# A transformer layer on one core: first row's transposes and weight pieces, last group's softmax and residual loads moved

## The chip, the core and the metric

The kernel runs on one core of a Trainium2 chip. The core has a matrix engine (TensorE, PE in the profile; its weight loads are PEld), a vector engine (VectorE, DVE), an activation engine (ScalarE, ACT), a general engine (GpSimd, POOL) and a queue engine (SyncE, SP) that issues most of the transfers. The engines run side by side and wait for each other by semaphores; each works through its own list of instructions in order. [...]

The metric is the device time of one execution in microseconds (us), as the median of three runs. Besides, one execution was taken with the hardware profiler; it has a time of its own.

## The reference

The input `x` is 16 rows of 512 tokens with 512 features. Attention and a gated feed-forward part both read the same normalised input, and both are added to `x`:

```python
xn = layernorm(x)
q, k, v = split(xn @ w_qkv.T + b_qkv)              # 16 heads of 32
p = softmax(q @ k.T / sqrt(32) + causal)
attn = (p @ v) @ w_out.T + b_out
g = (xn @ gate_w.T) * gate_s                       # 1408 wide, weights -1, 0, 1
u = (xn @ up_w.T) * up_s
ffn = ((silu(g) * u) @ down_w.T) * down_s
out = x + attn + ffn
```

## The kernel before

Precision is kept by splitting float32 values into two float16 halves, a high one and the rest (`xh`, `xl`, `wq_h`, `wq_l`, `qkh`, `qkl`, `hh`, `hl`, `oh`, `ol`), so that each product is two or three matmuls of 128 x 512. ACT usually writes the high half, DVE or POOL the rest.

The 16 batch rows are handled one after the other, and in each the 16 heads in four groups of four. One group of one row is a slot: 64 slots, numbered 0 to 63. In a slot the softmax of the group runs (`soft_run`): PE computes scores in three blocks, for query tile 3, for tile 2, and for tiles 1 and 0 together, in four score banks (tag `s1`); DVE masks them and takes the maximum (L556), ACT the exponential (L561), ACT and DVE split the result (L581, L586), and SP issues DMA transposes of it (L595). In the next slot `av_step` multiplies with the values: PE spreads the reciprocal sums into a tile `R` (L628), ACT copies it to `Rs` (L631), PE does the product `av` (L641), DVE scales it (L654), ACT and POOL split it into `oh` and `ol` (L655, L656; five buffers each).

Between these, PE is filled with other work (`fillers`): the query and key projections of the next group (`qk_proj`, two tiles, out through ACT at L464), the value projections of a row, the chunks of the feed-forward part (`ffn_chunk`, a `g` and a `u` tile of eight matmuls each; chunks 0 to 2 in the first slot of a row, 3 and 4 in the second, 5 to 10 in the third), the four down tiles (`down_tile`, 22 matmuls each, fourth slot), and the four output tiles of the row before (`out_tile`, 12 matmuls each, second slot). These tiles share three PSUM banks (tag `mm`): a new tile can start when the third tile before it has been read. The output tiles of the last row (`ends`) start with three head groups and are finished with the fourth at the very end.

Who comes when is decided by a planner (`Plan.order`). Each step has an engine, a planned duration and the things that it reads and writes. PE takes, of the steps that can start, the one with the lowest key; keys are spread over the slot by `place`. The other engines take the one that has been ready longest, moved by its `slack` (a negative one makes it earlier). The outcome is one fixed list per engine. The table of planned times is used for nothing else.

At the start, SP loads the first row (four tiles of 256 KB) and the projection weights (twelve pieces of 256 KB: query, key and value part, four pieces of the contraction each, L263). DVE computes the statistics and normalises (L375 to L393), PE transposes the normalised row in four groups of four (`ln_tr`, L423) into `mm` banks, ACT and DVE split each group into `xh` and `xl` (L428, L431), and ACT and DVE split each weight piece (L270, L273). Then the projections of group 0 begin. For the later rows the transposes are done by DMA.

At the end of each row, `down_tile` brings a tile out of PSUM (L713), loads the residual again into a single buffer (`xr`, L716), and POOL adds the output bias to it and it to the tile (L717, L718). The output tile is then added on DVE (L739) and stored (L742).

## Time and profile before

| what | value |
|---|---|
| median of three runs | 1915.01 us (1914.96 to 1915.26) |
| the profiled execution's own time | 1915.52 us |
| its span, first to last instruction | 1913.7 us |
| PE, DVE, ACT, POOL busy | 98%, 77%, 70%, 51% of the span |
| first matmul (a transpose) of PE | 11.29 us |
| last matmul of PE | starts 1904.69 us |
| last instruction of DVE | starts 1905.18 us |

Times in the profile count from the start of the span. A row of the timeline has the start, the duration, the engine, the line and operation, what it writes and reads, how often, and in brackets how long the engine had idled and what ended it. Buffer numbers are left out, so `qk` stands for any projection tile. Matmuls overlap: the distance from start to start (about 0.22 us for 128 x 512 at full clock) tells the pace, not the duration. The granted clock is the clock that PE was allowed, 1.00 being full. POOL's spans are rough.

### The profile page before, as it was taken

What the parts mean: (1) busy time and instruction counts of PE and PEld (TensorE: products, weight loads), DVE (VectorE), ACT (ScalarE), POOL (GpSimd) and SP (SyncE); (2) the same over time, 40 slices, a digit from 0 to 9 for tenths busy, and PEclk for the clock granted to TensorE, in tenths of its full rate; (3) what the DMA queues carried; (4) which work ended last, traced back from release to release, by engine and by line L of the source; (5) the groups of instructions that cost most, each with busy time, mean ns of one, the idle gap of its engine ahead of it and who ended that gap; (6) DMA issues with size and microseconds to landing.
All of it is one profiled execution on the core that took longest, in us unless ns stands there. A gap on an engine that the chain in (4) does not pass through costs nothing. (4 is left out here: it accounts for less than half of the span.)

```text
span 1913.7 us, 40913 instructions
## 1 busy us (share of the span) xinstructions
PE 1877.3 (98%) x15250; PEld 892.2 (47%) x15250; DVE 1482.0 (77%) x3541; ACT 1335.2 (70%) x3185; POOL 983.5 (51%) x713
## 2 busy tenths in 40 slices
PE   7899999999999999999999999999999999999997
PEld 3344444444444444444444444444444444444443
DVE  7778778797887978878788787877869787686674
ACT  5766757677676776767767676776767767677673
POOL 4446455464554646456464554645546454564533
PEclk9999999999999999999999999999999999999999
DMA  9875757666676656767567586667766667666465
GB/s 169 144 127 120 133 128 154 129 130 121 132 153 128 145 109 138 143 135 144 110 133 144 122 148 123 139 121 140 153 127 135 119 136 148 127 130 106 97 118 115
DMA packets 769519, 252.39 MB, mean 132 GB/s; under 512 B 734368, under 2 KB 738848, under 8 KB 769312
## 3 DMA queue, kind: packets, MB, share of 16 engines
q1 hardware_dynamic: 764688, 247.54, 65.7%
q0 software_dynamic: 4624, 2.16, 1.4%
q8 instruction: 121, 1.98, 0.4%
q14 instruction: 86, 0.70, 0.1%
HBM read 55.85 MB, written 16.78 MB: 38 GB/s over the span
## 5 line engine op out<-in xcount | busy, mean ns | idle before, releaser
L561 ACT ACTIVATE p<-s,negm 128x512 f32<-128x512 f32 (+3 forms) x1024 | 529.0, 531 | 231.3 <-DVE negm L556 229.1
L586 DVE SCALAR_TENSOR_TENSOR pq<-p,pq 128x2048 f16<-128x2048 f32 (+3 forms) x256 | 425.7, 1676 | 238.5 <-ACT pq L581 229.2
L556 DVE CUSTOM_DVE_ANT_0 s<-s,mask 128x512 f32<-128x512 f32 (+3 forms) x1024 | 473.1, 517 | 53.0 <-PE s L527 45.2
L581 ACT ACTIVATE pq<-p 128x2048 f16<-128x2048 f32 (+3 forms) x256 | 324.0, 1291 | 10.3 <-DMA pT<-pq 8.4
L691 POOL TENSOR_TENSOR hl<-ft,hh 128x512 f16<-128x512 f32 x176 | 226.9, 1295 | 190.1 <-ACT hh L690 189.3
L469 POOL TENSOR_TENSOR qkl<-qkt,qkh 128x512 f16<-128x512 f32 x128 | 165.1, 1290 | 244.7 <-ACT qkh L467 233.9
L251 PE MATMUL g<-xh,wg 128*128 128x512 f16 x704 | 267.6, 380 | 4.3 <-ACT qkt L464 2.4
L251 PE MATMUL u<-xh,wu 128*128 128x512 f16 x704 | 266.9, 379 | 2.8 <-DVE ft L681 1.5
L251 PE MATMUL dn<-wd,hh 128*128 128x512 fp8e4 x704 | 268.2, 381 | 0.0
L251 PE MATMUL dn<-wd,hl 128*128 128x512 fp8e4 x704 | 267.4, 380 | 0.0
L251 PE MATMUL g<-xl,wg 128*128 128x512 f16 x704 | 266.9, 379 | 0.0
L251 PE MATMUL u<-xl,wu 128*128 128x512 f16 x704 | 266.8, 379 | 0.0
L690 ACT CAST hh<-ft 128x512 f16<-128x512 f32 x176 | 109.3, 622 | 170.5 <-DVE ft L687 170.3
L618 POOL TENSOR_SCALAR rb<-rden 128x512 f32<-128x512 f32 x64 | 137.7, 2151 | 175.9 <-DVE rden L615 175.9
L251 PEld LDWEIGHTS <-wu 128*128 128x128 fp8e4 x1408 | 137.1, 98 | 169.7 <-issue 5.6
L561 ACT ACTIVATION_READ_ACCUMULATOR p<-s,negm 128x1 f32 x1024 | 214.5, 209 | 0.0
L251 PEld LDWEIGHTS <-wg 128*128 128x128 fp8e4 x1408 | 132.6, 98 | 159.6 <-issue 10.3
L251 PEld LDWEIGHTS <-wq_h 128*128 128x128 f16 x1024 | 95.4, 98 | 133.8 <-issue 28.5
L677 ACT ACTIVATE ft<-g,gt_c 128x512 f32<-128x512 f32 x176 | 121.1, 688 | 43.7 <-PE g L251 43.1
L407 POOL TENSOR_TENSOR xnl<-xc,xnh 128x512 f16<-128x512 f32 x60 | 96.7, 1612 | 104.5 <-DMA xl<-xnl 58.4
L687 DVE SCALAR_TENSOR_TENSOR ft<-u,gu_c,ft 128x512 f32<-128x512 f32 x176 | 132.0, 750 | 21.4 <-PE u L251 5.5
L717 POOL TENSOR_TENSOR xr<-xr,bo_b 128x512 f32<-128x512 f32 x64 | 94.4, 1475 | 103.9 <-DMA xr<-in_x 103.9
(114 smaller groups left out, 3205.3 us busy)
## 6 DMA issues: line engine op xcount, KB each, us to landing
xc<-in_x SPq DMA_DIRECT2D x64, 256.0 KB, 4.0
xr<-in_x SPq DMA_DIRECT2D x64, 256.0 KB, 2.9
out<-y SPq DMA_DIRECT2D x64, 256.0 KB, 2.5
pT<-pq SPq DMA_TRANSPOSE x256, 5.5
wq<-in_wqkvT SPq DMA_DIRECT2D x12, 256.0 KB, 5.4
exact<-in_wdT SPq DMA_DIRECT2D x11, 256.0 KB, 2.9
exact<-in_wgT SPq DMA_DIRECT2D x8, 256.0 KB, 3.0
exact<-in_wuT SPq DMA_DIRECT2D x8, 256.0 KB, 2.9
```

The costliest lines, as they stand in the source:

```text
L251: nc.tensor.matmul(ps(), l, r, start=(first + k == 0), stop=(first + k == n - 1))
L407: add("POOL", gps(512), lambda: nc.gpsimd.tensor_tensor(l(), xc(), h(), ALU.subtract), r=[xc, h], w=[l], slack=2)
L469: "POOL", gps(512), lambda: nc.gpsimd.tensor_tensor(l(), t(), h(), ALU.subtract),
L556: nc.vector.tensor_tensor_reduce(sc, sc, mask[:, 512 - n :], -(2.0 ** -7), 3e38, ALU.add, ALU.min, negm()[:, m : m + 1])
L561: nc.scalar.activation(exps(i).rearrange("p (k j) q -> p k j q", j=4)[:, :, j, :], part().rearrange("p (k q) -> p k q", q=P), AF.Exp, bias ...
L581: "ACT", act(4 * n), lambda src=src, half=half: nc.scalar.mul(half(0), src(), 2.0 ** 15),
L586: lambda src=src, half=half: nc.vector.scalar_tensor_tensor(half(1), src(), 2.0 ** 15, half(0), ALU.mult, ALU.subtract),
L618: lambda: nc.gpsimd.tensor_scalar(rb().rearrange("p (c d) -> p c d", d=32), rden().unsqueeze(2).to_broadcast([P, 16, 32]), 2.0 ** -15, Non ...
L677: "ACT", act(512) + 0.1, lambda: nc.scalar.activation(t(), pg(), AF.Tanh, scale=gt_c[:, ic : ic + 1]),
L687: lambda: nc.vector.scalar_tensor_tensor(t(), pu(), gu_c[:, ic : ic + 1], t(), ALU.mult, ALU.mult),
L690: add("ACT", act(512), lambda: nc.scalar.copy(hh(), t()), r=[t], w=[hh], slack=3)
L691: add("POOL", gps(512), lambda: nc.gpsimd.tensor_tensor(hl(), t(), hh(), ALU.subtract), r=[t, hh], w=[hl])
```

## The change

1. `ln_tr` puts its four tiles into the score banks (tag `s1`, four of them) instead of the three `mm` banks, and its ACT and DVE steps get a slack of -8.
2. The query and key weights are loaded and split in two pieces each: first the 128 columns of group 0 for the whole contraction, then the other 384 columns. The value weights come in two pieces of two contraction tiles. There are six loads and six splits instead of twelve; the bias load comes after the first two. The projections wait for the pieces accordingly.
3. For the last row, only two output tiles of the row before are computed in its second slot, the other two in its fourth.
4. In the last slot the keys of the softmax steps are spread over 0.4 of the slot; the last `av` gets a key at 0.6 of it, ahead of the last parts of the output tiles, which begin at the end of the slot.
5. For the last row, the residual tiles lie in the row buffers (tag `xc`, four) instead of one buffer, and are loaded once slot 61 has begun instead of after the down tile.

In the lists that the planner makes, everything between the first projections and slot 61 is the same on every engine. PE's list from slot 61 on, with the number of matmuls (`s1_3`, `s1_2`, `s1_1` are score blocks; slot numbers where it matters):

```
before: av(60) op 8 s1_2 op 28 s1_1 op 8, g u 3 and 4 (32), s1_3(62) qk 24 flagT R av(61) flagR g u 5 ..
        .. g u 10, s1_3(63) R dn 30 av(62) dn 12 s1_2 dn 36 s1_1 dn 10 op 35 R av(63) op 12
after:  av(60) s1_2 op 20 g 4 s1_1 g 4 u 8 g u 4 (16) qk 12 s1_3(62) qk 12 R g 5 s1_2 flagT u 5 av(61) flagR ..
        .. g u 10, s1_3(63) op 24 s1_2 R dn 8 av(62) dn 8 s1_1 dn 50 R dn 22 op 9 av(63) op 27 op 12
```

```diff
-    def load_wqkv(part, kc, t):
+    def load_wqkv(part, k, t, cols, kcs=slice(0, KC)):
+
+        src = wqkvT[kcs.start * P : kcs.stop * P, part * 512 + cols.start : part * 512 + cols.stop]
         add(
             "SP", 0.5,
-            lambda: nc.sync.dma_start(t()[:, kc, :], wqkvT[kc * P : (kc + 1) * P, part * 512 : part * 512 + 512]),
-            w=[(t, kc)], lat=1.3,
-        )
...
+            lambda: nc.sync.dma_start(t()[:, kcs, cols], src.rearrange("(k p) f -> p k f", p=P)),
+            w=[(t, k)], lat=5.2 * (cols.stop - cols.start) * (kcs.stop - kcs.start) / 2048,
+        )
...
+        h, l = wq_h[:, kcs, dst], wq_l[:, kcs, dst]
+        add("ACT", act(n), lambda: nc.scalar.mul(h, t()[:, kcs, cols], 256.0), r=[(t, k)], w=[("wqh", part, k)])
...
+            lambda: nc.vector.scalar_tensor_tensor(l, t()[:, kcs, cols], 256.0, h, ALU.mult, ALU.subtract),
+            r=[(t, k), ("wqh", part, k)], w=[("wql", part, k)], slack=4,
...
-        ps = mm(f"lnT_{b}_{kc}")
+        ps = Tile(pp, [P, 512], F32, "s1", 4, f"lnT_{b}_{kc}")
...
-        add("ACT", act(512), lambda: nc.scalar.copy(xh()[:, kc, :], ps()), r=[ps], w=[(xh, kc)])
+        add("ACT", act(512), lambda: nc.scalar.copy(xh()[:, kc, :], ps()), r=[ps], w=[(xh, kc)], slack=-8)
...
-            r=[ps, (xh, kc)], w=[(xl, kc)],
+            r=[ps, (xh, kc)], w=[(xl, kc)], slack=-8,
...
-                    [(wt, which, kc)] + xtok(b, xx, kc),
+                    [(wt, which, min(g, 1))] + xtok(b, xx, kc),
...
-                    [(wt, 2, kc)] + xtok(b, xx, kc, tb),
+                    [(wt, 2, kc // 2)] + xtok(b, xx, kc, tb),
...
-        xr = work(f"xr_{b}_{tb}", "xr", 1)
+
+        xr = work(f"xr_{b}_{tb}", "xr", 1) if b + 1 < NB else work(f"xr_{b}_{tb}", "xc", 4)
...
-        add("SP", 0.5, lambda: nc.sync.dma_start(xr(), x[b, tb * P : (tb + 1) * P, :]), r=[y], w=[xr], lat=1.3)
+        add(
+            "SP", 0.5, lambda: nc.sync.dma_start(xr(), x[b, tb * P : (tb + 1) * P, :]),
+            r=[y] if b + 1 < NB else [f"slot{NSLOT - 3}"], w=[xr], lat=1.3,
+        )
...
-                step.key = t0 + AV_LAG + (k - 1) * 1.5
+                step.key = t0 + AV_LAG + (k - 1) * 1.5 if s < NSLOT else t0
...
-        if g == 1 and b > 0:
-            for tb in range(NT):
+
+        late = 2 if b == NB - 1 else NT
+        if b > 0 and g in (1, 3):
+            for tb in range(late) if g == 1 else range(late, NT):
                 out_tile(f, b - 1, tb)
...
-    for part in range(3):
-        for kc in range(KC):
-            load_wqkv(part, kc, wst[part])
-        if part == 1:
+    first, others, both = slice(0, P), slice(P, 512), slice(0, 512)
+    pieces = [(0, 0, wst[0], first), (1, 0, wst[1], first), (0, 1, wst[0], others), (1, 1, wst[1], others)]
+    pieces += [(2, k, wst[2], both, slice(2 * k, 2 * k + 2)) for k in range(2)]
+    for n, piece in enumerate(pieces):
+        load_wqkv(*piece)
+        if n == 1:
             add("SP", 0.5, lambda: nc.sync.dma_start(bqk_c, bqk), w=["bqk"], lat=0.3)
...
-    for part in range(3):
-        for kc in range(KC):
-            split_wqkv(part, kc, wst[part])
+    for piece in pieces:
+        split_wqkv(*piece)
...
-        place(start, T)
+
+        place(start, T if s + 1 < NSLOT else 0.4 * T)
         f.place(start, T)
+        early = start + 0.6 * T
...
-    attention_slot(NSLOT)(start, 0.0)
+    attention_slot(NSLOT)(early, 0.0)
...
-    f.place(start + AV_LAG + 4.0, f.total)
+    f.place(start, f.total)
```

More of the change, by code (lines that the diff above doesn't have):

```diff
@@ L257, in mm_group, with split_wqkv @@
             prev = [f.pe(MM4 / 4 * (k1 - k0), lambda k0=k0, k1=k1: run(k0, k1), reads, [ps], prev)]
-    def load_wqkv(part, kc, t):
+    def load_wqkv(part, k, t, cols, kcs=slice(0, KC)):
+        src = wqkvT[kcs.start * P : kcs.stop * P, part * 512 + cols.start : part * 512 + cols.stop]
         add(
             "SP", 0.5,
-            lambda: nc.sync.dma_start(t()[:, kc, :], wqkvT[kc * P : (kc + 1) * P, part * 512 : part * 512 + 512]),
-            w=[(t, kc)], lat=1.3,
-        )
-    def split_wqkv(part, kc, t):
-        cols = slice(part * 512, part * 512 + 512)
-        h, l = wq_h[:, kc, cols], wq_l[:, kc, cols]
-        add("ACT", act(512), lambda: nc.scalar.mul(h, t()[:, kc, :], 256.0), r=[(t, kc)], w=[("wqh", part, kc)])
-        add(
-            "DVE", dve(512),
-            lambda: nc.vector.scalar_tensor_tensor(l, t()[:, kc, :], 256.0, h, ALU.mult, ALU.subtract),
-            r=[(t, kc), ("wqh", part, kc)], w=[("wql", part, kc)],
+            lambda: nc.sync.dma_start(t()[:, kcs, cols], src.rearrange("(k p) f -> p k f", p=P)),
+            w=[(t, k)], lat=5.2 * (cols.stop - cols.start) * (kcs.stop - kcs.start) / 2048,
+        )
+    def split_wqkv(part, k, t, cols, kcs=slice(0, KC)):
+        n = (cols.stop - cols.start) * (kcs.stop - kcs.start)
+        dst = slice(part * 512 + cols.start, part * 512 + cols.stop)
+        h, l = wq_h[:, kcs, dst], wq_l[:, kcs, dst]
+        add("ACT", act(n), lambda: nc.scalar.mul(h, t()[:, kcs, cols], 256.0), r=[(t, k)], w=[("wqh", part, k)])
+        add(
+            "DVE", dve(n),
+            lambda: nc.vector.scalar_tensor_tensor(l, t()[:, kcs, cols], 256.0, h, ALU.mult, ALU.subtract),
+            r=[(t, k), ("wqh", part, k)], w=[("wql", part, k)], slack=4,
         )
@@ L776, in weight_exact @@
         )
-    rng_src = [(wq_h, kc, 512 * k, ("wqh", k, kc)) for k in range(3) for kc in range(KC)]
-    rng_src += [(wo_h, kc, 0, ("woh", kc)) for kc in range(KC)]
+    rng_src = [(wq_h, kc, 512 * k, [("wqh", k, 0), ("wqh", k, 1)]) for k in range(3) for kc in range(KC)]
+    rng_src += [(wo_h, kc, 0, [("woh", kc)]) for kc in range(KC)]
     rng_cols = {38: (0, 4), 39: (4, 8), 40: (8, 12), 41: (12, 16), 35: (16, 28), 36: (28, 40), 37: (40, 51)}
@@ L788, in weight_range @@
             ),
-            r=[tok] + when, w=["ranges"], slack=8,
+            r=tok + when, w=["ranges"], slack=8,
         )
```

## The prediction

> **What bounds the kernel now.** I read the page's busy rows first, then who TensorE waited for, then the order of time at both ends, then the granted clock by stretches.

> ```profile
> PE 1877.3 (98%) x15250; PEld 892.2 (47%) x15250; DVE 1482.0 (77%) x3541; ACT 1335.2 (70%) x3185; POOL 983.5 (51%) x713
> ```

> TensorE (PE) is the bound: it works in all but 36 us of 1913.7. So the change is worth what it takes from PE's idle or slow time.

> ```profile
> PE lnT L423 <- DVE xc L393: 11.3, 1, 11.3
> PE R L628 <- POOL rb L618: 2.9, 1, 2.9
> PE g L251 <- ACT qkt L464: 2.4, 1, 2.4
> PE op L251 <- ACT oh L655: 1.5, 1, 1.5
> PE op L251 <- POOLq L1113: 1.3, 1, 1.3
> PE lnT L423 <- DVE xl L431: 0.8, 1, 0.8
> ```

> These are PE's waits over the span (total, times, longest). The 0.8 is at the head, 1.5 and 1.3 are at the tail; 2.9 and 2.4 lie between, where the order is untouched.

> ```profile
> 14.84 1.28 DVE L431 TENSOR_TENSOR xl<-lnT,xh 128x512 f16<-128x512 f32 x2
> 15.57 1.12 PE L423 MATMUL lnT<-ident,xc 128*128 128x128 f32 x4 [0.82 <-DVE xl L431]
> 16.48 1.91 PE L251 MATMUL qk<-xh,wq_h 128*128 128x512 f16 x4
> 18.19 1.80 PE L251 MATMUL qk<-xl,wq_h 128*128 128x512 f16 x4
> 19.83 1.03 PE L251 MATMUL qk<-xh,wq_l 128*128 128x512 f16 x4
> ```

> The head. The fourth transpose group waits 0.82 us for VectorE (DVE) to free the first of three banks. The next eight matmuls start 0.43 us apart, and from 19.83 on 0.22 apart: PE runs at half speed until about 19.7.

> ```profile
> 1897.82 0.29 PE L641 MATMUL av<-pT,vh 128*32 128x256 f16 x4 [0.85 <-DMA pT<-pq]
> 1900.85 0.39 PE L251 MATMUL op<-wo_h,oh 128*128 128x512 f16 x1 [1.52 <-ACT oh L655]
> 1902.74 0.39 PE L251 MATMUL op<-wo_h,ol 128*128 128x512 f16 x1 [1.29 <-POOLq L1113]
> 1903.24 2.63 DVE L739 SCALAR_TENSOR_TENSOR y<-op,y 128x512 f32<-128x512 f32 x4 [3.10 <-PE op L251]
> ```

> The tail: three waits on the last group's softmax, transposes and split, 0.85 + 1.52 + 1.29 = 3.66 us. After them come twelve matmuls, four additions and the stores.

> ```profile
> 57.24:60.65 3.41, 1.75 (x11) 0.96 (x9) 2.58 (x6) 3.00 (x6) 1.51 (x2) 1.00 0.65 146
> 111.85:115.26 3.41, 0.85 (x4) 0.20 (x2) 3.41 (x8) 1.07 (x4) 1.59 (x2) 1.00 0.27 52
> 115.26:118.67 3.41, 3.05 (x10) 1.59 (x11) 2.73 (x6) 3.41 (x8) 1.43 (x2) 0.51 0.00 0
> ```

> Stretches (PE's busy us first, granted clock third from the end). After a stretch in which PE worked 25%, the clock is 0.51 for 3.4 us; after one of 51% it stays 1.00.

> **The change, part by part: the head.** The four transpose groups get the four score banks, so the wait goes. The third group ends near 14.75; the fourth starts there instead of at 15.57, and the first projection matmul at 15.69 instead of 16.48. Gain 0.8, if its data keep up: group four ends 15.87, ScalarE's (ACT) copy (0.58) 16.5, DVE's difference (0.68) 17.2; matmuls four and eight need them at 17.0 and 18.7 at half speed. DVE is ready, because seven weight splits ahead of and between the four differences became two.

> The loads: 4 MB of input and weights still pass, cut otherwise. The two first pieces have runs of 512 B. Here 256 KB with 2 KB runs took about 0.65 us once flowing (390 GB/s at 9 to 12 us). [...] the pieces, issued from 2.62 on and landing 4.8 to 6.2 after issue, are there at 8 to 10 us. No row here shows a plain 512 B load; if a run cost as much as one of 2 KB, each piece took 2.6 and the second landed at 11.7. ACT needs both split (0.63 each) before its copy at 13.08. So both ends cost nothing and I take nothing. The slack that covers this is under 1 us at the late end; past it, each us is a us on PE. The other pieces are needed from 16.5 on (a 128x1536 ACT split 1.48, DVE 1.76 each), and PE asks for them after 21: hidden. A bias load moves up one place; it is needed at 12.5.

> The half-speed stretch is the open term. [...] 115.26 lies 28.0 windows after 19.69, and the clock's fall at 1907.26 lies 553.0 after it. So the window that opened it was 16.28 to 19.69; the one before (12.87 to 16.28) had the 0.82 hole in it and was 76% busy. With the hole closed it is full, mostly of transposes, and neither page nor trace says what a transpose counts. If it opens at 16.28, eight matmuls take 8 x 0.2155 + 0.3 = 2.0 instead of 3.35: head gain 0.8 + 1.3 = 2.1. If not, the opening stays at 19.69 and the earlier start only adds slow time: gain 0.4. By the row alone (0.43 for the first eight matmuls, wherever they start) it would be 0.8. I take 2.1.

> Two later stretches hang on the same windows, since everything behind the head shifts by its gain. Shifted by 2.1, PE's 2.9 us hole at 112.7 to 115.6 spreads over two windows (about 60% and 54% busy): the slow stretch would go, worth half of its 3.05 busy us, 1.5. But the 2.4 hole at 59.0 to 61.4 then leaves 43% in its window, between the 51% that stayed open and the 36% (1903.85 to 1907.26) after which it closed: up to 1.7 lost. I count the two as zero and keep -1.5 and +1.7.

> **The tail.** Half of the previous row's output tiles (24 matmuls, 24 x 0.2155 = 5.2 us) move from slot 61 into slot 63, between the last group's first and second score blocks; slot 63's blocks come in 0.4 of its length; the last av goes behind the last down tile and nine output matmuls, ahead of 27 others. Counting from the last group's first scores: second block at 6.0, third at 12.6, its exponentials (ACT 3.2 in all) done by about 19, both DVE splits (1.25 + 0.68) by 22.2, transposes landed 5.0 later as at the end of this trace (1892.7 to 1897.7), at 27. PE reaches av at 31.5: no wait (0.85 gone, 4 us to spare). Then 0.68 + 0.62 + 1.15, with hand-overs 2.9 us, lie beside 27 x 0.2155 = 5.8 of PE: 1.52 and 1.29 gone. Gain 3.66.

> What comes late instead is slot 62. With 5.2 us less PE work in slot 61, ACT falls behind. In the order that the planner writes out for the changed kernel, PE has there, from the end of slot 61's av (1815.98) to u of chunk 5, 84 matmuls (18.1), four score blocks (0.69 + 0.70 + 0.85 + 0.69) and two transposes (0.7): it arrives at 1837.7. That tile's bank is held by the second projection of the last group, freed by ACT (L464). ACT is fed last by PE's u of chunk 3 (DVE done 1826.1), then has a projection to wait for (1831.4), 0.72 + 0.51 + 0.52 + three exponentials 0.67, Rs 0.5, one more 0.8, the 128x2048 scaling 1.81 and the projection's own 0.70:

> ```profile
> 1839.30 1.94 ACT L581 ACTIVATE pq<-p 128x2048 f16<-128x2048 f32 x1
> 1841.11 0.70 ACT L464 ACTIVATE qkt<-qk,bqk_c 128x512 f32<-128x512 f32 x1
> ```

> (There 1.81 from start to start.) It ends at about 1839.1, so PE waits about 1.4 (0.5 to 2.9). Queued behind it: u, av, chunk 6. From there on ACT and DVE are ahead again. One or two more switches between kinds of matmul, 0.1 at each side: 0.2.

> Residuals: four loads move from the last group's transfers to slot 61 and into row buffers that are free since slot 56. On SP's queue they stand ahead of slot 61's transposes, whose data come 8 us later; on POOL four additions (1.3 to 1.5) stand ahead of a projection split that PE needs 14 us later (done 1817.7, needed 1831). Two stores stand ahead of the last group's transposes and are due 4 us before them. ACT's `oh` of group 1 now waits for the moved tiles' reads (five buffers), about 4.2 us into slot 63, where ACT is at 4.4. Each costs nothing; POOL's cover is 13 us.

> Sum: head -2.1, windows 0, tail -3.66 + 1.4 + 0.2 = -2.0: -4.1. From the profiled execution's 1915.52 (its span 1913.7) that is 1911.4; the median of the runs lies 0.5 below it: **1910.9**.

> **Rivals.** (1) The clock opens at 19.69 as before: head -0.4, total -2.4, 1912.6. For it: transposes start 0.28 apart[...]. Against: the stretch from 115.26 reopened the clock with R's transposes in it. (2) The wait in slot 62 takes the place of those at the end: if ACT is 3.5 late rather than 1.4, the tail gives nothing, and with the head's 2.1 it is 1912.9. For it: ACT has no idle time there; against: every term is a measured row. (3) Slower: the first pieces land late. ACT is in order, its copy of the first transpose stands behind the second split, and PE behind the copy. Each us after 12.4 costs one; from 16.5 it eats the gain, from 20.3 the kernel is over 0.2% slower (1919). Against: that is eight times what the row gives for the bytes.

> **Chances.** Main case 0.52, (1) 0.33, (2) 0.10, (3) 0.05. Tell-apart bound 0.2% = 3.8 us. The main case passes it in about seven of ten (its own range 1909.0 to 1912.6), (1) in one of seven, (2) in one of ten: faster 0.44, slower 0.06 with (3), within it 0.50. Range: down to 1908.3 (both windows' gain, no wait in slot 62), up to 1914.6 ((1) or (2) with the long wait).

> **What would show it.** No wait of the transposes on `xl`, first projection matmul near 15.7; starts 0.22 apart from 16.3, or from 19.7; the granted clock near 57 and 115. In slot 62 a wait of u on `qkt` of 1 to 2 us; no waits of av or op at the end, and the last matmul 4 us earlier. Wrong if the first pieces land after 12.4, or if slot 61 to 63 holds other waits of over 1 us.

## The result and the profile after

The changed kernel takes 1909.15 us (median of ten executions, 1906.54 to 1911.35), the kernel before, on the same chip, 1914.95 us (1912.92 to 1915.53). The ratio of the two is 0.9972 (95% interval 0.9962 to 0.9982), so the gain is 5.4 us, 3.4 to 7.3. The profiled execution's own time is 1909.74 us and its span 1908.0 us. A second series with the same kernel gave 0.9970 (0.9958 to 0.9982).

The busy row of the page and the waits of TensorE over the span (total, times, longest):

```profile
PE 1877.7 (98%) x15250; PEld 893.3 (47%) x15250; DVE 1485.7 (78%) x3535; ACT 1334.9 (70%) x3179; POOL 986.7 (52%) x713
```

```profile
PE lnT L426 <- DVE xc L396: 10.1, 1, 10.1
PE g L251 <- ACT qkt L467: 3.3, 1, 3.3
PE R L631 <- POOL rb L621: 2.9, 1, 2.9
PE u L251 <- ACT qkt L467: 2.7, 2, 1.7
```

PE's busy time has not moved (1877.3 before): the gain is idle time. The waits on `xl`, on `oh`, on `ol` and on the last `pT` are gone from the list. The wait of `g` has grown from 2.4 to 3.3, and `u` waits 2.7 in two places, 1.7 of it in slot 62. The first matmul starts at 10.1 instead of 11.3; how much of that is chance is said below.

The head in order of time:

```profile
10.09 4.22 PE L426 MATMUL lnT<-ident,xc 128*128 128x128 f32 x16 [10.09 <-DVE xc L396]
14.15 1.21 PE L251 MATMUL qk<-xh,wq_h 128*128 128x512 f16 x4
15.20 1.02 PE L251 MATMUL qk<-xl,wq_h 128*128 128x512 f16 x4
16.06 1.03 PE L251 MATMUL qk<-xh,wq_l 128*128 128x512 f16 x4
```

Sixteen transposes run without a gap, and the projections are at full clock (four in 0.86) from 15.2 on; before, this began at 19.83.

Slot 62 and the end, from the same view:

```profile
1833.66 1.91 ACT L584 ACTIVATE pq<-p 128x2048 f16<-128x2048 f32 x1
1835.47 0.67 ACT L467 ACTIVATE qkt<-qk,bqk_c 128x512 f32<-128x512 f32 x1
1836.19 0.38 PE L251 MATMUL u<-xh,wu 128*128 128x512 f16 x1 [1.65 <-ACT qkt L467]
...
1890.80 0.29 PE L644 MATMUL av<-pT,vh 128*32 128x256 f16 x4
...
1893.47 0.62 ACT L658 CAST oh<-Rs 128x512 f16<-128x512 f32 x1 [8.62 <-DVE Rs L657]
...
1894.16 1.16 POOL L659 TENSOR_TENSOR ol<-Rs,oh 128x512 f16<-128x512 f32 x1 [3.17 <-ACT oh L658]
...
1899.31 2.63 DVE L746 SCALAR_TENSOR_TENSOR y<-op,y 128x512 f32<-128x512 f32 x4 [5.88 <-PE op L251]
1900.03 2.27 SPq L749 DMA_DIRECT2D out<-y  x4
```

The new wait of `u` is 1.65 us, behind the 128x2048 scaling and the projection's exit. At the end `av` has no bracket, so no wait of it shows. `oh` and `ol` are done at 1895.3; of PE's 39 output matmuls after `av` only the last twelve need them, and these start near 1898.4. The table of stretches (PE's busy us first, granted clock third from the end):

```profile
55.06:58.47 3.41, 0.19 (x1) 0.00 (x0) 3.26 (x8) 3.00 (x8) 2.18 (x2) 1.00 0.62 130
58.47:61.88 3.41, 3.33 (x8) 1.16 (x8) 3.20 (x12) 3.41 (x10) 1.25 (x2) 0.50 0.91 169
109.67:113.08 3.41, 0.49 (x4) 0.28 (x4) 3.41 (x10) 1.65 (x5) 1.82 (x2) 1.00 0.03 6
113.08:116.49 3.41, 3.41 (x12) 1.42 (x11) 2.08 (x4) 3.41 (x7) 0.79 (x1) 0.50 0.05 10
1833.40:1836.81 3.41, 1.76 (x17) 0.71 (x17) 2.22 (x9) 3.38 (x6) 0.00 (x0) 1.00 0.41 77
1836.81:1840.22 3.41, 3.41 (x30) 1.43 (x32) 3.41 (x4) 3.38 (x10) 2.35 (x1) 0.50 0.00 0
```

Three stretches of 3.41 us run at half clock, each after one with a wait in it. The kernel before had one, at 115. The third comes behind the new wait in slot 62.

### The profile page after: what moved, and what is told of

It reads as the page before. It is cut to its first block, busy times and chain, and to the rows that moved or that the text cites. A ratio compares the mean times of both kernels' runs of the same rounds, so it can differ in the third digit from the quotient of the medians.

```text
span 1908.0 us, 40895 instructions
## 1 busy us (share of the span) xinstructions
PE 1877.7 (98%) x15250; PEld 893.3 (47%) x15250; DVE 1485.7 (78%) x3535; ACT 1334.9 (70%) x3179; POOL 986.7 (52%) x713
## 5 line engine op out<-in xcount | busy, mean ns | idle before, releaser
L251 PE MATMUL g<-xh,wg 128*128 128x512 f16 x704 | 268.4, 381 | 5.0 <-ACT qkt L467 3.3
L251 PE MATMUL u<-xh,wu 128*128 128x512 f16 x704 | 267.4, 380 | 4.5 <-ACT qkt L467 2.7
L251 PE MATMUL dn<-wd,hh 128*128 128x512 fp8e4 x704 | 268.3, 381 | 0.0
L251 PE MATMUL g<-xl,wg 128*128 128x512 f16 x704 | 267.8, 380 | 0.0
L251 PE MATMUL dn<-wd,hl 128*128 128x512 fp8e4 x704 | 267.6, 380 | 0.0
L251 PE MATMUL u<-xl,wu 128*128 128x512 f16 x704 | 267.6, 380 | 0.0
L251 PEld LDWEIGHTS <-wu 128*128 128x128 fp8e4 x1408 | 137.5, 98 | 171.6 <-issue 8.1
L251 PEld LDWEIGHTS <-wg 128*128 128x128 fp8e4 x1408 | 132.9, 98 | 160.9 <-issue 12.3
L251 PEld LDWEIGHTS <-wq_h 128*128 128x128 f16 x1024 | 95.1, 98 | 132.9 <-issue 26.7
L659 POOL TENSOR_TENSOR ol<-Rs,oh 128x512 f16<-128x512 f32 x64 | 98.8, 1544 | 96.7 <-ACT oh L658 96.6
```

The costliest lines, as they stand in the source:

```text
L251: nc.tensor.matmul(ps(), l, r, start=(first + k == 0), stop=(first + k == n - 1))
L659: add("POOL", gps(512), lambda: nc.gpsimd.tensor_tensor(ol(), r(), oh(), ALU.subtract), r=[r, oh], w=[ol])
```

## The experiments

Each kernel was timed beside the kernel before. The ratio is its time to that kernel's time. Line numbers in the profile of an experiment are those of its own text and differ from the changed kernel's by a few.

| kernel | median us | before us | ratio (95%) |
|---|---|---|---|
| e1_head | 1911.07 | 1913.89 | 0.9985 (0.9979 to 0.9992) |
| e2_tail | 1911.32 | 1913.89 | 0.9985 (0.9978 to 0.9991) |
| e3_banks | 1911.17 | 1913.89 | 0.9986 (0.9979 to 0.9993) |
| e4_pieces | 1913.35 | 1913.89 | 0.9996 (0.9988 to 1.0004) |
| e5_residual | 1913.88 | 1913.54 | 1.0004 (0.9995 to 1.0012) |
| e6_no_late | 1909.85 | 1913.54 | 0.9981 (0.9974 to 0.9988) |
| e7_no_keys | 1912.83 | 1913.54 | 0.9999 (0.9991 to 1.0007) |
| e8_chunk | 1907.21 | 1913.54 | 0.9971 (0.9959 to 0.9982) |
| f_after | 1909.47 | 1913.91 | 0.9970 (0.9958 to 0.9982) |
| e9_warm | 1907.19 | 1913.91 | 0.9962 (0.9949 to 0.9976) |
| e10_both | 1904.89 | 1913.91 | 0.9946 (0.9933 to 0.9960) |
| e11_all | 1902.06 | 1913.91 | 0.9936 (0.9922 to 0.9949) |

The profiles let two lengths be read apart from the rest: from the first transpose to the first scores (the head), and from a projection matmul of slot 61 (at 1811.1 in the kernel before) to the last matmul (the tail).

| kernel | first transpose | clock opens behind it | head | half-clock stretches | tail | last matmul to end of span |
|---|---|---|---|---|---|---|
| before | 11.29 | 8.45 | 15.54 | 115 | 93.59 | 9.0 |
| after | 10.09 | 4.00 | 12.98 | 58, 113, 1837 | 93.04 | 7.2 |
| f_after | 10.81 | 3.39 | 12.70 | 59, 113, 1837 | 93.03 | 7.4 |
| e1_head | 10.80 | 5.05 | 13.31 | 60 | 93.53 | 7.0 |
| e2_tail | 10.99 | 8.28 | 15.45 | 115, 1839 | 93.09 | 7.9 |
| e3_banks | 10.30 | 4.83 | 14.06 | 60 (two), 1899 | 95.17 | 7.0 |
| e4_pieces | 11.06 | 4.04 | 15.12 | none | 93.67 | 8.9 |
| e5_residual | 10.31 | 4.93 | 13.25 | 60, 114 | 90.94 | 12.6 |
| e6_no_late | 10.39 | 6.51 | 14.03 | 112 (two) | 92.53 | 7.9 |
| e7_no_keys | 10.96 | 6.45 | 13.99 | 113 (two) | 94.02 | 6.8 |
| e8_chunk | 9.99 | 4.74 | 13.15 | 59, 114 | 89.58 | 6.7 |
| e9_warm | 10.25 | 5.70 | 13.25 | 13, 112 | 91.40 | 7.3 |
| e10_both | 10.37 | 5.17 | 13.25 | 12, 111 (two) | 89.58 | 8.9 |
| e11_all | 10.50 | 5.56 | 13.25 | 13 | 89.58 | 8.7 |

Half-clock stretches are given by the time at which they begin, "(two)" where it lasts 6.83 us and not 3.41. In the last three kernels the clock had opened before the first real transpose and closed again (below); the table has its second opening. Up to slot 61 PE's order is the same in all kernels but e3_banks, the added transposes aside.

**Head and tail, each alone**

```diff
 e1_head: changes 1 and 2 (banks with their slack, pieces); the rest as before
 e2_tail: changes 3, 4 and 5 (moved output tiles, keys, residuals); the rest as before
```

> The head alone (score banks, pieces, slack); the tail as before. Theory: the head gives 1.2 us (the row's third tile lands earlier), 0.8 (the wait on xl) and about 1.5 (TensorE's full clock one window of 3.41 us earlier), less what later slow windows take: 1911.5 us (1910.5 to 1912.7), first transpose near 10.1, no slow wait in slot 62. Rival, only the wait counts: -0.8, 1914.1. Rival, the gain is the tail's: 1914.9.

> The tail alone (late output tiles, early keys and av, residuals in the row buffers); the head as before. Theory: 3.66 us of waits at the end go, a wait of u on qkt of 1.4 to 1.7 in slot 62 comes, sometimes with a slow clock window after it (up to 1.7): -1 to -2.3, 1912.6 to 1913.9. Rival, the head gives only its 0.8 and the tail the rest: -5, 1910. Rival, the new wait and window eat the tail's gain: 1914.9.

Head alone gives 2.9 us (1.5 to 4.0), tail alone 2.9 (1.7 to 4.2), together 5.8 against 5.4 for the whole. The two halves add, and neither carries the gain by itself. The rivals by which one half gives nothing fall.

**The head taken apart**

```diff
 e3_banks: twelve loads and splits as before, and
-        ps = mm(f"lnT_{b}_{kc}")
+        ps = Tile(pp, [P, 512], F32, "s1", 4, f"lnT_{b}_{kc}")
 with slack=-8 on the ACT and DVE steps behind
 e4_pieces: the six loads and splits, the transposes in the mm banks and without the slack
```

> The score banks and the slack for the first row's transposes alone, with the twelve weight loads as before. Theory: the wait on xl goes (0.8), first transpose still near 11.3, the window without the hole opens the clock earlier in part of the executions: -0.8 to -2.1, 1912.9 to 1914.1. Rival, the twelve weight splits in ACT's and DVE's lists make the projections wait in place of the transposes: 1914.9.

> The weight pieces alone, the transposes in the three banks as before. Theory: the pieces with runs of 512 B leave the row's third and fourth tile more of the transfer rate, so that the third statistic starts near 5.2 instead of 6.5 and the first transpose near 10.1; the wait on xl stays or shrinks: -1.2, 1913.7 (1912.7 to 1914.2). Rival, the earlier landing was chance: first transpose near 11.3, 1914.9.

By the timing the banks with their slack give as much as the whole head (0.9986 against 0.9985), and the pieces alone nothing that can be measured. But e3_banks is not the banks alone: with the twelve loads the planner orders PE's work otherwise from 22 to 118 us, and there the waits differ too (`R` on `rb` 5.8 us in three places, no wait of `g` on ACT). What is clean in it is the start: no wait on `xl`, and the first projection 4.10 us behind the first transpose, as with the pieces; of its head of 14.06, 0.86 are four matmuls that stand behind the first scores elsewhere. My expectation for the pieces named a cause that fell at once: the third statistic of the row started at 6.24 in e4_pieces and at 5.48 in e3_banks, which has the old loads. So the pieces are not what decides when the row lands. The first transpose starts at 10.30 to 11.29 in the three profiles with twelve loads and at 9.99 to 11.06 in the others. The pieces alone do take the wait on `xl` away, but two others come in its place (e4_pieces in order of time):

```profile
15.04 1.49 ACT L273 ACTIVATE wq_h<-wq 128x1536 f16<-128x1536 f32 x1
15.19 0.81 PE L251 MATMUL qk<-xh,wq_h 128*128 128x512 f16 x3
16.42 0.58 ACT L431 CAST xh<-lnT 128x512 f16<-128x512 f32 x1
16.89 2.44 ACT L273 ACTIVATE wq_h<-wq 128x1536 f16<-128x1536 f32 x2
17.05 0.38 PE L251 MATMUL qk<-xh,wq_h 128*128 128x512 f16 x1 [1.05 <-ACT xh L431]
...
18.97 0.38 PE L251 MATMUL qk<-xl,wq_h 128*128 128x512 f16 x1 [0.90 <-DVE xl L434]
```

ACT takes a 1.49 us split of a large piece ahead of the fourth copy, and PE's fourth and eighth matmul wait for it. In the whole change the slack of -8 puts that split behind the copy. Slack and banks were not tried apart from each other.

**The tail taken apart**

```diff
 e5_residual: the whole change, but
-            r=[y] if b + 1 < NB else [f"slot{NSLOT - 3}"], w=[xr], lat=1.3,
+            r=[y], w=[xr], lat=1.3,
 and xr in its one buffer for every row
 e6_no_late: the whole change, but the four output tiles stay in slot 61
 e7_no_keys: the whole change, but keys of softmax and last av as before
```

> All of the change but the residual buffers: the last row's residuals are loaded after the down tiles into the one buffer again. Theory, the residual part is worth nothing (additions and loads lie beside TensorE): as the whole change, about 5.3 us below the kernel before (4.5 to 6). Rival: POOL's additions come behind the last down tiles and hold the last y, which the end waits for: 1 us or more is lost, seen as a later DVE addition at the end and not as a wait of TensorE.

> All of the change but the moved output tiles: slot 61 keeps its four. Theory, the wait of u on qkt in slot 62 (1.7) comes from that move alone and goes, the clock's slow window behind it (up to 1.7) too, and the three waits at the end stay away, since seventeen output matmuls (3.7 us) still stand behind the last av: 1.7 to 3.4 faster than the whole change, 7 to 8.7 us below the kernel before. Rival, the two moved tiles are needed as cover between the last group's score blocks: waits of s and av of 2 us or more come back and it is no faster than the whole change.

> All of the change but the softmax's keys in the last slot: late output tiles and residual buffers stay, the last softmax and av are placed as before. Theory, the keys take the waits at the end away: with them undone op waits for oh and ol again (1.5 and 1.3), and the wait in slot 62 stays (1.7): 2.8 to 3.7 slower than the whole change, 1.6 to 2.5 us below the kernel before. Rival, the moved output tiles alone give the softmax the time: under 1 us slower than the whole change.

e5_residual: the expected nothing was wrong by the whole gain. Its last matmul is early (1898.86), but the span ends 12.6 us later. SP's queue, POOL and DVE at the end:

```profile
1893.37 1.27 POOL L720 TENSOR_TENSOR xr<-xr,bo_b 128x512 f32<-128x512 f32 x1
1894.72 1.26 POOL L721 TENSOR_TENSOR y<-y,xr 128x512 f32<-128x512 f32 x1
1898.13 0.99 SPq L745 DMA_DIRECT2D out<-y  x2
1899.21 0.41 SPq L719 DMA_DIRECT2D xr<-in_x  x1
1899.71 7.29 SPq L745 DMA_DIRECT2D out<-y  x2
1903.31 1.26 POOL L720 TENSOR_TENSOR xr<-xr,bo_b 128x512 f32<-128x512 f32 x1 [7.33 <-DMA xr<-in_x]
1904.65 1.26 POOL L721 TENSOR_TENSOR y<-y,xr 128x512 f32<-128x512 f32 x1
1905.95 0.69 DVE L742 SCALAR_TENSOR_TENSOR y<-op,y 128x512 f32<-128x512 f32 x1 [6.55 <-POOL y L721]
```

The fourth residual load stands on SP's queue behind two output stores, which wait for the finished output tiles. Its buffer is free from 1895.98 on, when POOL's addition ends, but it is issued at 1899.21, lands 4.1 later, and two additions on POOL stand before the last addition on DVE at 1905.95. The kernel before had its fourth load at 1895.64, ahead of all stores. The new order of the tail moves it behind them; the residual part of the change takes it out of the way, and is worth about 5 us there (12.6 against 7.2 and 7.4 behind the last matmul).

e6_no_late: 0.9981 (0.9974 to 0.9988), not faster than the whole change (0.9972, 0.9962 to 0.9982), where I expected 1.7 to 3.4 us; the intervals overlap, so it isn't shown to be slower either. The wait and the half-clock stretch in slot 62 are gone as expected, but PE waits in other places (its waits from 1808 on):

```profile
PE s L530 <- ACT p L564: 0.9, 3, 0.3
PE op L251 <- POOLq L1123: 0.6, 1, 0.6
PE op L251 <- ACT oh L658: 0.3, 1, 0.3
```

That is 1.8 us against 1.65: its tail of 92.53 is 0.5 shorter than that of the whole change with a half-clock stretch, and 1.1 longer than one without (91.40 in e9_warm). The moved tiles are cover for the score blocks, as the rival said, though for less than its 2 us. The two half-clock stretches at 112 in its profile lie ahead of the edit: up to slot 61 PE's order is that of the whole change.

e7_no_keys: 0.9999; I expected 1.6 to 2.5 us below the kernel before. The waits of 1.5 (`oh`) and 1.7 (slot 62) are both there, 0.6 on `ol` besides, and the tail is 94.02, longer than before. So moving the tiles without the keys costs 0.4 in the tail. With the head's 2.9 us (1.5 to 4.0) some 2.5 should remain; the timing shows 0.2, between 1.7 below the kernel before and 1.3 above. The two only just agree (1.1 to 3.6 should remain). Where the rest went stays open; the two half-clock stretches near 113 are in this profile, but in e6_no_late's too.

**What else the traces point to**

```diff
 e8_chunk: the whole change, and in fillers
-        for ic in range(CUTS[g], CUTS[g + 1]):
+        cuts = CUTS if b + 1 < NB else (0, 3, 6, IC, IC)
+        for ic in range(cuts[g], cuts[g + 1]):
 e9_warm: the whole change, and ahead of ln_tr
+    warm = Tile(pp, [P, 512], F32, "s1", 4, "warm")
+    def warm_up():
+        for _ in range(38):
+            nc.tensor.transpose(warm()[:, 0:P], ident, ident)
+    add("PE", 7.0, warm_up, w=[warm], key=-1.0)
 e10_both: e8_chunk and e9_warm together
 e11_all: e10_both, and in load_wo, for DVE's step
-            r=[t, ("woh", kc)], w=[("wol", kc)], slack=8.0,
+            r=[t, ("woh", kc)], w=[("wol", kc)], slack=20.0,
```

> The whole change, and in the last row chunk 5 of the feed-forward part goes from slot 62 into slot 61, in the place of the moved output tiles. Theory, slot 61 is long enough again for ACT to catch up: the wait of u on qkt in slot 62 shrinks below 0.5 us and no slow window follows; no waits at the end: 1.2 to 3.4 faster than the whole change, 6.5 to 8.7 us below the kernel before. Rival, ACT stays behind because chunk 5 brings its own ACT work along: a wait of over 1 us elsewhere in slots 61 and 62, no gain.

> The changed kernel again, beside the next three on one chip, as their measure: 0.9972 of the kernel before (0.9962 to 0.9982). Its first row lands by chance anywhere in 1.2 us, so first transpose at 10.0 to 11.3; the first scores 13.0 to 14.1 behind it.

> The whole change, and 38 transposes of the identity on TensorE from about 2 us on, before the first row is there (they compute nothing that is used). Theory, transposes count as work for the clock: it opens before 9 us, the sixteen real transposes go 0.14 apart instead of 0.28 and no matmul is slow; the copies behind them then set the pace (0.85 each), so of 16 x 0.14 = 2.2 only a part is left: first scores 11.8 to 12.7 behind the first transpose instead of 13.0 to 14.1, 0.6 to 1.8 us faster than the changed kernel. Rival, the clock opens for matmuls only: it stays at half until 14 or later, no difference. Rival, the added transposes delay the real ones: up to 0.8 slower.

> The former kernel with, besides, chunk 5 of the last row in slot 61. Theory, the two add: the 1.7 us wait in slot 62 and the slow window that sometimes follows it go too: 1.5 to 2.5 us faster than the kernel with the added transposes alone. Rival, the slot-62 wait was hidden by what follows: no difference.

> The former kernel, and DVE takes the reciprocal of the third group's sums ahead of the splits of the output weights (their slack 20 instead of 8), so that the wait of R on rb near 112 us (2.9) goes. Theory, with the wait the slow clock window behind it goes (1.7 in those executions where the wait lies in one window): 2.9 to 4.6 faster than the former kernel. Rival, only the wait is saved and something else is late: 0 to 2 faster.

e8_chunk: from slot 61 on PE shows no wait at all, and the tail is 89.58, here and in e10_both and e11_all: 1.8 shorter than the whole change without the half-clock stretch, 3.5 shorter than with it. The timed ratio (0.9971) doesn't show it against 0.9972, but the two were not timed side by side; e10_both against e9_warm, on one chip, gives 2.3 in the medians, with intervals that overlap.

e9_warm: 2.3 us below f_after in the medians, with intervals that overlap, and not by the mechanism that I expected. PE in order of time, and the stretches:

```profile
1.84 6.24 PE L919 MATMUL warm<-ident 128*128 128x128 f32 x38 [1.84 <-POOL ident masks.py:199]
10.25 3.57 PE L426 MATMUL lnT<-ident,xc 128*128 128x128 f32 x16 [2.17 <-DVE xc L396]
13.61 1.92 PE L251 MATMUL qk<-xh,wq_h 128*128 128x512 f16 x4
```

```profile
2.30:5.71 3.41, 3.41 (x18) 3.41 (x17) 1.82 (x5) 0.00 (x0) 0.00 (x0) 1.00 0.99 334
5.71:9.13 3.42, 2.37 (x22) 2.13 (x20) 3.04 (x15) 1.26 (x2) 0.00 (x0) 1.00 1.09 341
9.13:12.54 3.41, 1.91 (x11) 1.34 (x12) 3.31 (x11) 0.56 (x2) 0.00 (x0) 1.00 1.06 380
12.54:15.95 3.41, 3.41 (x13) 1.92 (x12) 2.98 (x8) 3.14 (x6) 0.00 (x0) 0.50 1.05 354
```

(Up to the clock's first record, at 5.71 here, the column says 1.00 though the pace is lower: 18 transposes in 3.41 us before it, 22 in 2.37 us behind it.) The clock opened at 5.71 by transposes alone, as the theory said. But it closed again at 12.54: the stretch before had transposes in 1.91 of its 3.41 us only, since the row came at 10.25. The first scores start 13.25 behind the first real transpose, not 11.8 to 12.7. The trace's gain over f_after comes at 57 us, where `g` waits 1.2 instead of 3.4, since ACT is released by the transfers 2.2 us earlier; only 0.6 of this is explained by the weight loads having been issued earlier. What speeds the transfers stays open.

e11_all: 1902.06 us, 2.8 below e10_both in the medians (the intervals overlap), at the lower end of the theory. DVE takes the reciprocal at 106.05 instead of 110.5, the wait of `R` on `rb` (2.9 in every kernel above but e3_banks) is no longer among the waits of the span, and no stretch near 112 is at half clock. The longest waits after those of the start are now:

```profile
PE u L251 <- DVE ft L684: 1.7, 4, 0.7
PE g L251 <- ACT qkt L467: 1.6, 1, 1.6
PE g L251 <- DVE y L746: 1.3, 1, 1.3
```

It is faster than both kernels of this document: 11.9 us below the kernel before, 7.4 below the changed one on the same chip.

## Why the prediction was right

The forecast was 1910.9 us, 4.1 below the profiled execution of before, by 2.1 in the head and 2.0 in the tail. Measured: 5.4 (3.4 to 7.3), the head alone 2.9 (1.5 to 4.0), the tail alone 2.9 (1.7 to 4.2). Both forecasts lie within their intervals. Each term is held against the runs below. Some were wrong in their mechanism, and that the sum still holds is in part luck.

**Banks.** Right. The wait on `xl` is gone, and the first projection follows the first transpose by 3.8 to 4.1 us instead of 5.2.

**The clock.** Right in size, with luck, and wrong in how firmly it was placed. Rival (1) needed the clock to open when it did before; it opens 3.4 to 6.5 us behind the first transpose in the seven profiles that have the whole change of the head (after, f_after, e1, e5 to e8), against 8.3 and 8.5 in the two with the old head. The seven heads are 13.3 long on average, the two old ones 15.5: 2.2 us, against a forecast of 2.1. But the clock changes on a grid of windows of 3.413 us (last section), and this lies differently from one execution to the next: in after and f_after, the same kernel, it opens 4.00 and 3.39 us behind the first transpose. The forecast that it opens behind the first full window was the author's estimate from a single opening, at 19.69 (behind 3.41 us of work, and not behind 2.59 in the window before). So 16.28 was one draw of many, and the old head is known from two draws only. What a transpose counts was left open there. The runs tell a part: a window filled by transposes opened the clock (after: 14.09, ahead of the first projection), and so did the added transposes alone in e9_warm (5.71), but one that they filled to 91% or 89% didn't, though they had no gap (e6_no_late, e7_no_keys: it opened a window later, at 16.90 and 17.41).

**"Everything behind the head shifts by its gain."** This step failed. The kernel before, and then the changed one, at the feed-forward weights' first load, where ACT goes on, and at the wait of `g`:

```profile
25.99 0.98 POOL L293 DMA_DIRECT2D wg<-in_wgT  x1
56.98 1.58 ACT L581 ACTIVATE pq<-p 128x1024 f16<-128x1024 f32 x2 [4.76 <-DMA pT<-pq]
61.40 0.38 PE L251 MATMUL g<-xh,wg 128*128 128x512 f16 x1 [2.41 <-ACT qkt L464]
```

```profile
22.84 0.99 POOL L296 DMA_DIRECT2D wg<-in_wgT  x1
54.12 1.57 ACT L584 ACTIVATE pq<-p 128x1024 f16<-128x1024 f32 x2 [5.64 <-DMA pT<-pq]
58.55 0.59 PE L251 MATMUL g<-xh,wg 128*128 128x512 f16 x1 [3.30 <-ACT qkt L467]
```

The kernel before is 3.8 us behind at 24 us and only 2.9 when `g` starts (against f_after 3.3 and 2.4). `g` waits for ACT, and ACT for transposes by DMA that land behind the 2.2 MB of feed-forward weights. Those loads stand on POOL behind the split of the first projections; in the eleven kernels without added transposes ACT goes on 31.0 to 31.6 us after the first of them is issued. So the head's gain counts there by what it brings forward that issue (25.99 to 22.84), and a longer wait stands in between. That the loads set this distance is inferred from its being so constant; no run moved them alone.

**Windows counted as zero.** The stretch at 115 did not go (it came back at 113), and the one at 58 newly closed, as the forecast's +1.7. But that loss did not last: against the kernel before, the changed one is 2.85 us ahead where `g` starts, 1.6 at 61 and 2.85 again from 69 on. The kernel before waits for ACT behind `g` (0.45 at 63.73, 0.60 and 0.30 at 72), the changed one only 0.30. In other executions the stretches lay otherwise, from none (e4_pieces) to three.

**Loads and pieces cost nothing.** Right, with banks and slack: the two first pieces, in runs of 512 B, land a median of 4.5 us behind their issue in after (before, in runs of 2 KB: 5.4 over the twelve pieces), and ACT splits them from 6.97 and 7.86 on, long before 12.4, so rival (3) fell. Their cover is not only time but order: e4_pieces shows 1.05 + 0.90 where ACT's order is not protected, a case that the prediction did not name.

**Slot 62.** The wait of `u` was forecast at 1.4 (0.5 to 2.9) and measured 1.65, with the same two ACT instructions last. It doesn't eat the tail's gain as in rival (2): the tail alone gives 2.9. Missed was what it can do to the clock: in after, f_after and e2_tail the 3.41 us behind it run at half clock, in e5_residual (where the wait is 1.4), e9_warm and e7_no_keys they don't. From start to start of the same matmuls e9_warm is 2.48 us ahead of f_after when the same wait of 1.65 ends and 4.11 once f_after's clock is back; e5_residual goes from 0.66 to 2.29. So the stretch costs 1.63.

**The end.** Right: 0.85, 1.52 and 1.29 are gone. The tail is 93.59 before, 91.40 (e9_warm) and 90.94 (e5_residual) without the half-clock stretch, 93.0 with it: 2.2 to 2.7 or 0.5, against a forecast of 2.0, which had no term for that stretch.

**Residuals "cost nothing".** As a cost, right. But the step said nothing of what the rest of the tail would do without them: about 5 us lost, with the last load behind two stores on SP's queue (e5_residual). The forecast's tail counted PE's waits only; the last load was safe only because this edit was in the change.

**What stays open.** 1.3 us between 4.1 and 5.4, which lie within the interval. The two profiles alone can't settle it. Their 5.7 us are 1.2 of an earlier first transpose, 2.6 of head, -0.4 between head and tail, 0.5 of tail and 1.8 behind the last matmul. The first of these (9.99 to 11.29 over all kernels) and the last (6.7 to 9.0, with both tails; e5_residual apart) vary by as much between kernels that don't differ there, and e2_tail is 1.07 us ahead of the kernel before at 1811, though PE's order is the same up to there. So the shares of head and tail rest on the timed halves and on the lengths in the table, not on this one pair.

## What to carry to other kernels

A gain at PE is worth what the next wait lets through: ask of every later wait whether its end is set by PE or by something that was started from a fixed point, such as a block of weight loads. A short wait on TensorE cost twice here in after and f_after, once itself (1.65 us) and once as a half-clock window behind it (1.63 us), while a later wait took up the loss of the window at 58 in after (2.85 us ahead of the kernel before, then 1.6, then 2.85 again). The wait went by moving work between neighbouring slots (e8_chunk: a tail of 89.58 without it). And an edit that costs and brings nothing alone may be what another edit stands on: undo each part within the whole, not only on the kernel before.

## What the hardware showed

How full a window must be, the traces show in part. With the clock full, it closed in before and after behind every window that was busy for 34% or less (23% and 34% in before, 6%, 14% and 0% in after), and behind none of 55% or more. In other profiles it closed behind 0% (e3_banks, from 56.09) up to 41% (e10_both, 1.40 us from 107.70), and behind two windows of transposes at 52% and 56% (e11_all, 1.77 us from 9.24; e9_warm, 1.91 us from 9.13). In between it went both ways: it stayed behind 44% and 52% in before (1.50 us from 1897.08, 1.77 us from 1900.49), and closed behind 52% in slot 62 of after and f_after (1.76 us each). This window of e9_warm, with the same wait in it and the same 1.76 us of work, left it open, and the one in e7_no_keys with this wait (1.7) did, too:

```profile
1831.84:1835.25 3.41, 1.76 (x16) 0.68 (x8) 2.76 (x9) 3.41 (x6) 0.00 (x0) 1.00 0.43 82
```

So the busy time alone doesn't decide. The window of after holds a whole score block (12 matmuls of 32 rows), the wait behind it and three matmuls of `u` (128 rows); that of e9_warm holds the end of a score block, the wait, and six matmuls of `u`. Which of these differences counts was not tried.

With the clock at half, these three stretches bear on the other border, from e6_no_late, from e2_tail and from before:

```profile
10.08:13.49 3.41, 3.10 (x12) 2.37 (x13) 3.41 (x10) 1.04 (x2) 0.00 (x0) 1.00 1.07 387
```

```profile
114.84:118.25 3.41, 2.73 (x9) 1.56 (x10) 2.89 (x6) 3.41 (x9) 1.76 (x2) 0.50 0.00 0
```

```profile
115.32:118.73 3.41, 3.11 (x10) 1.65 (x11) 2.67 (x6) 3.41 (x8) 1.36 (x2) 0.50 0.00 0
```

The first, all transposes, is 91% busy and didn't open the clock (it opened at 16.90, one window later). The second and the third, four transposes of `R` with five and six matmuls of `dn`, are 80% and 91% busy and did. Mixed windows of 67 to 75% didn't (2.30 us in e3_banks from 59.50, 2.53 in e6_no_late from 112.47, 2.57 in e7_no_keys from 112.98), and the half-clock stretch doubled. One of 99% transposes did (3.39 us in f_after, 10.79 to 14.20). That a transpose counts less than a matmul is the author's estimate from these few windows (91% that didn't against 80% and 91% that did), and was not tried by itself.
